# A norm summed in four column groups and spread by DMAs, and a silu gate, in a 16-stage network on one core

## The chip, the core and the metric

The kernel runs on one core of a Trainium2 chip. The metric is the device time of one execution in microseconds. The kernel before takes 4268.84 us, the median of three runs (4268.18 to 4270.52).

## The reference, cut to what matters

The reference sends an activation `x` of 16 sequences x 256 positions x 128 features, in fp32, through 16 residual stages: `x = x + stage(layernorm(x))`. The stages are, in order: a linear attention, a local layer, performer, the local layer again, linear, mixture of experts, decay, mixture of experts, causal linear, mix, window, mix, rope, adapters, ssm, adapters. Two of them matter here.

The local stage runs twice in the network, and each run has two layers:

```python
for layer in range(2):
    q, k, v = split(shift_token(x) @ wqkv)
    x = x + local_attention(rotary(l2norm(q)), rotary(l2norm(k)), v) @ wo   # windows of 64, the one before seen too
    h = shift_token(x)
    h = (h - h.mean(-1)) / sqrt(h.var(-1) + 1e-05) * lg + lb
    a, g = split(h @ w1 + b1)
    x = x + (a * gelu(g)) @ w2 + b2
```

The window stage is an attention with a sink (one more logit for each head in the softmax), and eight dense experts:

```python
h = h + attention(rmsnorm(h) * attn_norm_scale, sinks)
x = rmsnorm(h) * moe_norm_scale
gate = clip(gate_up[..., :INTER], NEG, 7.0);  up = clip(gate_up[..., INTER:], -7.0, 7.0)
out = sum over experts e of score[e] * ((up + 1) * gate * sigmoid(1.702 * gate)) @ down[e]
```

Every norm needs, for each position, a sum of squares over the 128 features.

## The kernel before, in words

Activations lie transposed in SBUF: the 128 features on the partitions and the 4096 positions along the free axis, in eight chunks of 512 (`NCH` is 8, `CH` is 512). Residual `x`, and the work arrays `ha` and `hb`, stay in SBUF for the whole program. All matmuls are fp32; the profile shows each of them as two passes, so it counts two matmuls for one call.

**A norm** has three steps, which the stages place where they like. `centre_step` (L1759) multiplies a chunk by the matrix `cent` and so subtracts the mean; the squares go to tile `nsq`, by GpSimd or by ScalarE. `spread_step` (L1774) multiplies `nsq` by the matrix `mean`, all of whose elements are 1/128. That sums over the partitions and at the same time leaves the sum on all 128 partitions. ScalarE then takes Ln and Exp(-0.5 x) of the whole 128x512 tile; the result is `nrs`, the factor 1/sqrt(variance + eps), on all partitions. With `twice` it makes two factors from one sum. The third step is a product on VectorE. `norm_x_step` (L1811) and `norm_of_half` (L3572) wrap these steps.

**The local layer** (`local_layer`, L3354) first calls `fill_rooms`, then `local_attend` and `local_ffn`. `local_attend` works through 32 half-sequence units, `m`; its order on each engine is the one written out in the loop at L3549 (`manual_schedule` keeps the emission order of every engine). One turn of `m` is called a slot here. `chunk_steps(m)` puts the norm steps in: for chunk c, `norm_of_half` does centre, spread, scale and bias in slots 4c+6 to 4c+9, for c below 7. In the first of two layers `norm_x_step` runs in slots 4c-9 to 4c-7, and only for chunks 5 to 7: the stage before has done the first five (`lead`, L1836). PSUM is shared as three banks `w`, four `s` and one `o`. `local_ffn` does the norm of chunk 7 in its turns 0 to 3 and then leads the next stage's norm.

**The rooms.** Both mixture-of-experts stages sort tokens into DRAM. `fill_rooms` (L2114) fills this memory once: 66 DMAs of up to 520 KB each and one of 64 KB, all issued by SP at the start of the first local layer.

**The window stage** (`window_attention`, L3163) has 128 units, n; the loop at L3327 starts at n = -14 with nothing but the norm of chunk 0. `before(c, i)` norms chunk c ahead of its projections, in slots 16c-14, 16c-12 and 16c-10, with two factors; `after(c, i)` norms the result for the experts, in slots 16c+24, +26 and +28. `prepare(0, 0)`, the first projections, comes at n = -8. Then `window_moe` (L2547) runs 64 units, eight experts for each of eight chunks: `wide` makes gate and up, `gate` multiplies them and the share `rb`, which ScalarE has copied from PSUM in `shares`, and `narrow` multiplies by `down`.

Weight loads for the next stage are issued by SP (`ahead`, L618) at the start of each stage and wait until the stage before is done with their buffer.

Of the kernel before, what the change touches and what calls it, by code (L numbers as in the profile page):

```python
# [1649 lines left out]
class Fast(Net):  # L1650
# [120 lines left out]
            self.gt(sq, dst, dst, ALU.mult)  # L1771
        return sq

    def spread_step(self, pool, sq, bank, eps="eps5", twice=False):  # L1774


        pv = self.bank(bank)
        self.mm(pv, self.k["mean"], sq)
        out = []
        for n in range(2 if twice else 1):  # L1780
            rs = pool.tile([P, CH], F32, tag=f"nrs{n}", name="nrs", bufs=2)
            if n:
                self.act(rs, pv, AF.Ln, scale=1.0 + 1e-5, bias=self.k["eps10"])
            else:
                self.act(rs, pv, AF.Ln, bias=self.k[eps])
            out.append(rs)
        for rs in out:
            self.act(rs, rs, AF.Exp, scale=-0.5)
        return out if twice else out[0]

    def norm_steps(self, pool, src, dst, bank, g=None, b=None, eps="eps5", copy=None, square=False):


        held = {}

        def centre():
            held[0] = self.centre_step(pool, src, dst, bank, copy, square)

        def spread():
            held[1] = self.spread_step(pool, held[0], bank, eps)  # L1800

        def scale():
            if g is None:
                self.tt(dst, dst, held[1], ALU.mult)
            else:
                self.stt(dst, dst, g, held[1], ALU.mult, ALU.mult)
                self.ts(dst, dst, b, ALU.add)

        return [centre, spread, scale]

    def norm_x_step(self, pool, c, i, bank="ps", copy=None):  # L1811

        if c in self.led:
            return
        if i == 0:
            s = self.chunk(c)
            self.norms[c] = self.norm_steps(pool, self.x[:, s], self.ha[:, s], bank, copy=copy)
        self.norms[c][i]()

    def slots(self, n, *steps, last=(), every=1):  # L1820
# [280 lines left out]
    def rooms(self, st):  # L2101


        nc = self.nc
        self.rows, self.many, self.filled = [], 0, False
        dram = st.enter_context(self.tc.tile_pool(name="dram", bufs=1, space=bass.MemoryType.DRAM))
        turns = sum(n == "moe_f" for n in self.loads)
        total = 8 * NT + WIDE
        for n in range(turns):
            self.rows.append(dram.tile([total, ROW], F32, tag=f"rows{n}", name="rows"))  # L2110
        if turns:
            self.back = dram.tile([2 * NT, C], F32, tag="back", name="back")

    def fill_rooms(self, st):  # L2114

        nc = self.nc
        if self.filled or not self.rows:
            return
        self.filled = True
        k = 8  # L2120
        t = self.stage(st, "fill", 1).tile([P, k, ROW], F32, tag="t", name="t")
        nc.gpsimd.memset(t, 0.0)
        nc.gpsimd.memset(t[:, :, C : C + 1].bitcast(I32), NOBODY)
        for rows in self.rows:
            n = rows.shape[0]
            for at in range(0, n, P * k):
                m = min(P * k, n - at) // P
                nc.sync.dma_start(rows[at : at + P * m].rearrange("(p a) d -> p a d", p=P), t[:, :m])
        nc.sync.dma_start(self.back[:P], t[:, 0, :C])

    def swiglu_moe(self, w):
        s = self.sending or self.send()
# [414 lines left out]
    def window_moe(self, w, h, n1):  # L2547

        x, nc = self.x, self.nc
        with ExitStack() as st:  # L2550
            p = self.stage(st, "e2", 1)
            compare, choose, turn = self.route_steps(st, w["gate"], 4, 0.25, w["gate_b"], "r")

            ub = p.tile([P, 16], F32, tag="ub", name="ub")
            self.ts(ub, w["gub"], 1.0, ALU.add)
            rts, rbs, gs, us, pos = {}, {}, {}, {}, {}

            def compared(c):
                self.logs(False)
                compare(c, n1)  # L2560

            def turned(c):
                rts[c] = turn(c)

            def shares(i):
                c, half = divmod(i, 2)
                rb = p.tile([P, 4, CH], F32, tag="rb", name="rb", bufs=2)
                for r, pb in enumerate(self.four(rts[c], self.k["sel4" + "ab"[half]], "r")):
                    self.act(rb[:, r], pb, AF.Copy)
                rbs[i] = rb  # L2570

            def wide(i):
                c, e = divmod(i, 8)
                s = self.chunk(c)
                pg, pu = self.bank(), self.bank()
                self.mm(pg, w["gu"][:, e * 256 : e * 256 + P], n1[:, s])
                self.mm(pu, w["gu"][:, e * 256 + P : e * 256 + 256], n1[:, s])
                g = p.tile([P, CH], F32, tag="g", name="g", bufs=4)
                u = p.tile([P, CH], F32, tag="u", name="u", bufs=6)
                sg = p.tile([P, CH], F32, tag="sg", name="sg", bufs=3)  # L2580
                self.ts(g, pg, w["gub"][:, 2 * e : 2 * e + 1], ALU.add, 7.0, ALU.min)
                self.act(sg, g, AF.Sigmoid, scale=1.702)
                self.ts(u, pu, ub[:, 2 * e + 1 : 2 * e + 2], ALU.add, 8.0, ALU.min)

                self.gt(g, g, sg, ALU.mult)
                gs[i], us[i] = g, u

            def gate(i):
                c, e = divmod(i, 8)
                self.stt(us[i], us[i], -6.0, gs.pop(i), ALU.max, ALU.mult)  # L2590
                self.gt(us[i], us[i], rbs[i // 4][:, e % 4], ALU.mult)

            def narrow(i):
                c, e = divmod(i, 8)
# [568 lines left out]
    def window_attention(self, w, h, n1, ns2):  # L3163
# [3 lines left out]
        with ExitStack() as st:  # L3167
# [134 lines left out]
            def before(c, i):  # L3302
# [2 lines left out]
                if i == 0:  # L3305
                    held["sq"] = self.centre_step(p1, self.x[:, s], h[:, s], "s", square=True)
                elif i == 1:
                    held["rs"] = self.spread_step(p1, held["sq"], "s", twice=True)
                else:
                    r1, r2 = held["rs"]  # L3310
                    self.stt(n1[:, s], h[:, s], w["ns1"], r2, ALU.mult, ALU.mult)
                    self.tt(h[:, s], h[:, s], r1, ALU.mult)

            def after(c, i):
# [3 lines left out]
                    held["sq"] = p1.tile([P, CH], F32, tag="nsq", name="nsq", bufs=2)  # L3318
                    self.act(held["sq"], h[:, s], AF.Square)
                elif i == 1:  # L3320
                    held["rs"] = self.spread_step(p1, held["sq"], "s")
                else:
                    self.stt(n1[:, s], h[:, s], ns2, held["rs"], ALU.mult, ALU.mult)

            with self.share(s=4, o=4), self.tc.manual_schedule():
                self.logs()
                for n in range(-14, len(units) + 16):  # L3327
                    if 0 <= n < len(units):
                        score(n)
                        later(n + 1, masked, n)  # L3330
# [10 lines left out]
                    i, rest = divmod(n - 14, 8)  # L3341
                    if rest == 0 and 0 <= i < 2 * NCH:
                        out(i)
                    c, u = divmod(n + 14, 16)
                    if u in (0, 2, 4) and c < NCH:
                        before(c, u // 2)
                    c, u = divmod(n - 24, 16)
                    if u in (0, 2, 4) and 0 <= c < NCH:
                        after(c, u // 2)

    def local_begin(self):
        pass
# [8 lines left out]
    def local_attend(self, w, z, hs, last):  # L3361
# [6 lines left out]
        with ExitStack() as st:  # L3368
# [158 lines left out]
            def chunk_steps(m):  # L3527
# [5 lines left out]
                if not last:  # L3533
                    for i in range(3):
                        if (c := due(i - 9)) is not None:
                            self.norm_x_step(p, c, i, "w")
                for slot in (-6, 5):
                    if (c := due(slot)) is not None:
                        self.shift(hs[:, self.chunk(c)], z[:, self.chunk(c)])
# [7 lines left out]
            with self.share(w=3, s=4, o=1), self.tc.manual_schedule():  # L3547
                self.logs()
                for m in range(-9, NTILE + 6):  # L3549
# [18 lines left out]
                    chunk_steps(m)  # L3568
                    if within(m + 5, NTILE):
                        project(m + 5)  # L3570

    def norm_of_half(self, pool, bank, w, s):  # L3572

# [3 lines left out]
            held[0] = self.centre_step(pool, s, s, bank)  # L3577

        def spread():
            held[1] = self.spread_step(pool, held[0], bank)  # L3580

        return [
            centre, spread, lambda: self.stt(s, s, w["lg"], held[1], ALU.mult, ALU.mult),
# [46 lines left out]
class Sending:  # L3630
# [3 lines left out]
    def __init__(self, net, rows):  # L3634
        self.net, self.rows, self.begun = net, rows, False
        self.stack = ExitStack()
        net.fill_rooms(self.stack)
        self.one = net.stage(self.stack, "g1", 1)
        self.p = net.stage(self.stack, "g2", 2)
        self.places = {-1: net.k["seg"]}  # L3640
# [208 lines left out]
```

## Time and profile before

| What | Value |
|---|---|
| Median of three runs | 4268.84 us |
| Profiled execution: its time / its span | 4291.23 us / 4289.4 us |
| Busy share of the span: PE, DVE, ACT, POOL | 91%, 61%, 54%, 45% |
| Mean granted TensorE clock | 0.949 |
| Local stage, its two runs, about | 115 to 840 us and 1130 to 1850 us of the span |
| Window attention, about | 2931 to 3407 us |
| Window experts, about | 3407 to 3654 us |

PE is TensorE's matmuls, PEld its weight loads, DVE VectorE, ACT ScalarE, POOL GpSimd and SP the engine that only issues DMAs. A row of the timeline gives start, duration, engine, line, operation, the tile written and the tiles read, the shape, a count when equal instructions are merged, and in brackets how long the engine was idle before it and what ended that. A matmul's shown duration includes the pipeline behind it, so the start of the next one says more than its end. A line such as L504 is a helper that many places call; the tile names say which place it is.

### The profile page before, as it was taken

How to read it: one execution, taken by the hardware profiler on the slowest of the kernel's cores; microseconds unless marked ns; L12 is line 12 of the kernel's file. 1: busy time of each engine (PE TensorE's matmuls, PEld its weight loads, DVE VectorE, ACT ScalarE, POOL GpSimd, SP SyncE). 2: the span in 40 equal slices, each digit the busy share in tenths (PEclk: the TensorE clock that was granted, in tenths of full speed). 3: DMA queues.
4: the chain of work that ended last, by engine and by line, in shares of the span. 5: the costliest groups of instructions: out<-in, count | busy, mean ns of one | idle time of the engine just before them, and what ended most of it. 6: DMA issues, size and time to landing. Idle time of an engine off the chain costs nothing. (4 is left out here: it accounts for less than half of the span.)

```text
span 4289.4 us, 73913 instructions
## 1 busy us (share of the span) xinstructions
PE 3886.8 (91%) x28998; PEld 2214.8 (52%) x28998; DVE 2597.7 (61%) x4503; ACT 2325.8 (54%) x4741; POOL 1949.6 (45%) x1696
## 2 busy tenths in 40 slices
PE   7999999998899999984989979888999999899978
PEld 3555466465465456553965549643444343455333
DVE  4775576374577377464336633555777698386474
ACT  6665466554766466552446634444555544674432
POOL 4664365232565166315433434454555498411251
PEclk8999999988999999997999979999999999999989
DMA  1800000000000000002930039100000000000000
GB/s 60 340 1 1 11 1 2 19 1 1 20 1 2 3 1 2 1 3 96 324 112 12 17 128 319 63 19 16 1 1 1 3 1 1 15 2 18 6 0 21
DMA packets 78404, 176.43 MB, mean 41 GB/s; under 512 B 12606, under 2 KB 39108, under 8 KB 77920
## 3 DMA queue, kind: packets, MB, share of 16 engines
q1 hardware_dynamic: 65568, 148.40, 10.0%
q0 software_dynamic: 9120, 18.51, 1.2%
q8 instruction: 231, 3.78, 0.4%
q10 hardware_dynamic: 3360, 4.72, 0.3%
q14 instruction: 125, 1.02, 0.1%
HBM read 118.28 MB, written 54.20 MB: 40 GB/s over the span
## 5 line engine op out<-in xcount | busy, mean ns | idle before, releaser
L528 ACT ACTIVATE pt<-ps 128x512 f32<-128x512 f32 x640 | 339.7, 600 | 325.1 <-PE ps L504 323.7
L504 PE MATMUL ps<-hb,w 128*128 128x512 f32 (+1 forms) x960 | 466.3, 619 | 8.8 <-issue 3.3
L504 PE MATMUL ps<-w,hb 128*128 128x512 f32 (+2 forms) x896 | 406.7, 575 | 25.4 <-DVE t L531 19.5
L534 POOL TENSOR_TENSOR t<-t,t 128x512 f32<-128x512 f32 x256 | 319.3, 1269 | 161.5 <-DVE t L531 101.5
L531 DVE TENSOR_TENSOR t<-ps,tab 128x512 f32<-128x512 f32 x512 | 317.6, 681 | 85.3 <-ACT sq L528 81.8
L534 POOL TENSOR_TENSOR t<-t,ss 128x1024 f32<-128x1024 f32 x128 | 243.5, 1903 | 218.7 <-ACT ss L528 217.5
L504 PEld LDWEIGHTS ps<-hb,w 128*128 128x128 f32 (+1 forms) x960 | 179.6, 192 | 270.5 <-issue 223.6
L528 ACT ACTIVATE qkt<-ps 128x512 f32<-128x512 f32 x256 | 140.5, 595 | 309.9 <-PE ps L508 309.3
L531 DVE TENSOR_TENSOR u<-u,ps 128x384 f32<-128x384 f32 (+1 forms) x206 | 121.8, 595 | 282.9 <-PE ps L504 122.4
L531 DVE TENSOR_TENSOR ot<-ps,rd 128x512 f32<-128x512 f32 (+2 forms) x224 | 143.3, 640 | 231.8 <-ACT rd L528 231.8
L534 POOL TENSOR_TENSOR nsq<-ha 128x512 f32<-128x512 f32 x112 | 123.1, 1099 | 322.0 <-ACT ha L528 305.0
L504 PEld LDWEIGHTS ps<-w,hb 128*128 128x128 f32 x896 | 156.8, 194 | 185.1 <-issue 115.4
L534 POOL TENSOR_TENSOR both<-pt 128x1024 f32<-128x1024 f32 x64 | 151.2, 2362 | 199.9 <-DVE pt L531 164.3
L504 PE MATMUL ps<-nsq,ct 128*128 128x512 f32 x368 | 203.6, 636 | 32.5 <-POOL nsq L534 27.6
L504 PE MATMUL ps<-ot,w 128*128 128x512 f32 x448 | 214.4, 613 | 17.3 <-DVE ot L531 9.2
L504 PE MATMUL ps<-u,w 128*128 128x512 f32 (+1 forms) x448 | 218.4, 611 | 8.4 <-POOL u L534 8.4
L2199 POOL DMA_INDIRECT back<-y,x x142 | 138.9, 978 | 185.5 <-ACT y L528 84.2
L504 PE MATMUL ps<-xt,w 128*128 128x128 f32 x1704 | 219.9, 279 | 1.7 <-ACT xt L528 1.5
L528 ACT ACTIVATE u<-ps,w 128x512 f32<-128x512 f32 x160 | 107.7, 685 | 183.1 <-PE ps L504 180.5
L504 PEld LDWEIGHTS ps<-xt,w 128*128 128x128 f32 x1704 | 203.7, 193 | 3.0 <-ACT xt L528 2.6
L3746 POOL DMA_INDIRECT rows<-out,idx x128 | 126.2, 986 | 170.2 <-ACT out L528 121.1
L528 ACT ACTIVATE nrs<-ps,ct 128x512 f32<-128x512 f32 x208 | 139.6, 683 | 103.2 <-PE ps L504 93.8
(363 smaller groups left out, 9095.3 us busy)
## 6 DMA issues: line engine op xcount, KB each, us to landing
w<-in_moe_x SPq DMA_DIRECT2D x142, 533.0 KB
rows<-t SPq DMA_DIRECT2D x64, 520.0 KB
x<-rows SPq DMA_DIRECT2D x142, 65.0 KB
w<-in_local_f SPq DMA_DIRECT2D x8, 659.5 KB
y<-back ACTq DMA_DIRECT2D x16, 256.0 KB
y<-back SPq DMA_DIRECT2D x16, 256.0 KB
w<-in_local_f SPq DMA_DIRECT2D x4, 658.5 KB
back<-y,x POOLq DMA_INDIRECT x142
```

Source lines behind the costliest of these rows:

```text
L504: self.nc.tensor.matmul(out, lhsT, rhs, start=start, stop=stop)
L528: self.nc.scalar.activation(out, in_, func, **kw)
L531: self.nc.vector.tensor_tensor(out, a, b, op)
L534: self.nc.gpsimd.tensor_tensor(out, a, b, op)
L2199: nc.gpsimd.indirect_dma_start(views[i], bass.IndirectOffsetOnAxis(ap=x[:, C : C + 1].bitcast(I32), axis=0), y, None, bounds_check=2 * NT ...
L3746: nc.gpsimd.indirect_dma_start(views[(c * 2 + k) * 4 + t], bass.IndirectOffsetOnAxis(ap=idx[:, k, t : t + 1], axis=0), out[:, k, t], None,)
```

## The change

Three things are changed.

First, `compact_spread`: the sum of squares is made by four matmuls with 32 columns of `mean`, each in its own column group of the array and each over a quarter of the chunk (128 positions). The quarter r lands on partitions 32r to 32r+31. ScalarE then takes Ln and Exp of 128x128 (of 128x128 twice and of 128x256 once with `twice`), into tile `nrow`. Four DMAs for each factor, issued by SP, read one row each, of partition 32r, and write it to all 128 partitions of `nrs`. It is used in the local layers (`norm_x_step` there, and `norm_of_half`) and in `before` and `after` of the window stage. The window's slots move: `before` in slots 16c-16, -14 and -10, `after` in 16c+24, +26 and +30, and the loop starts at n = -16.

Second, the DMAs that fill the rooms are put in a list, and SP issues two of them at the end of each slot of `local_attend`, in the first local layer.

Third, in the experts the gate is made by one Silu activation in place, silu(1.702 g) = 1.702 g sigmoid(1.702 g); the product on GpSimd and tile `sg` go away, and the factor 1/1.702 goes into the copy of `rb`.

```diff
+    def compact_spread(self, pool, sq, bank, eps, twice):
+        nc = self.nc
+        pv = self.bank(bank)
+        for r in range(4):
+            nc.tensor.matmul(
+                pv[32 * r : 32 * r + 32, :P], self.k["mean"][:, :32], sq[:, r * P : r * P + P],
+                start=True, stop=True, skip_group_check=True,
+            )
+        many = 2 if twice else 1
+        rows = pool.tile([P, many, P], F32, tag="nrow", name="nrow", bufs=2)
+        self.act(rows[:, 0], pv[:, :P], AF.Ln, bias=self.k[eps])
+        if twice:
+            self.act(rows[:, 1], pv[:, :P], AF.Ln, scale=1.0 + 1e-5, bias=self.k["eps10"])
+        flat = rows.rearrange("p n t -> p (n t)")
+        self.act(flat, flat, AF.Exp, scale=-0.5)
+        out = []
+        for n in range(many):
+            rs = pool.tile([P, CH], F32, tag=f"nrs{n}", name="nrs", bufs=2)
+            for r in range(4):
+                nc.sync.dma_start(rs[:, r * P : r * P + P], rows[32 * r : 32 * r + 1, n][:, None].broadcast_to([1, P, P]))
+            out.append(rs)
+        return out if twice else out[0]
...
-                nc.sync.dma_start(rows[at : at + P * m].rearrange("(p a) d -> p a d", p=P), t[:, :m])
-        nc.sync.dma_start(self.back[:P], t[:, 0, :C])
+                self.fills.append((rows[at : at + P * m].rearrange("(p a) d -> p a d", p=P), t[:, :m]))
+        self.fills.append((self.back[:P], t[:, 0, :C]))
+
+    def fill_some(self, n):
+        for out, t in self.fills[:n]:
+            self.nc.sync.dma_start(out, t)
+        del self.fills[:n]
...
-                    self.act(rb[:, r], pb, AF.Copy)
+                    self.act(rb[:, r], pb, AF.Copy, scale=1.0 / 1.702)
...
-                sg = p.tile([P, CH], F32, tag="sg", name="sg", bufs=3)
                 self.ts(g, pg, w["gub"][:, 2 * e : 2 * e + 1], ALU.add, 7.0, ALU.min)
-                self.act(sg, g, AF.Sigmoid, scale=1.702)
+                self.act(g, g, AF.Silu, scale=1.702)
                 self.ts(u, pu, ub[:, 2 * e + 1 : 2 * e + 2], ALU.add, 8.0, ALU.min)
-
-                self.gt(g, g, sg, ALU.mult)
...
-                for n in range(-14, len(units) + 16):
+                for n in range(-16, len(units) + 16):
...
-                    c, u = divmod(n + 14, 16)
-                    if u in (0, 2, 4) and c < NCH:
-                        before(c, u // 2)
+                    c, u = divmod(n + 16, 16)
+                    if u in (0, 2, 6) and c < NCH:
+                        before(c, (u + 1) // 3)
                     c, u = divmod(n - 24, 16)
-                    if u in (0, 2, 4) and 0 <= c < NCH:
-                        after(c, u // 2)
+                    if u in (0, 2, 6) and 0 <= c < NCH:
+                        after(c, (u + 1) // 3)
...
                     if within(m + 5, NTILE):
                         project(m + 5)
+                    self.fill_some(2)
+                self.fill_some(len(self.fills))
```

The calls of `spread_step` in `norm_x_step` of the local layer, in `norm_of_half`, and in the window's `before` and `after` get `compact=True`; all other norms stay as they were.

More of the change, by code (lines that the diff above doesn't have):

```diff
@@ L1772, in centre_step, with spread_step @@
         return sq
-    def spread_step(self, pool, sq, bank, eps="eps5", twice=False):
+    def spread_step(self, pool, sq, bank, eps="eps5", twice=False, compact=False):
+        if compact:
+            return self.compact_spread(pool, sq, bank, eps, twice)
         pv = self.bank(bank)
@@ L1789, in spread_step, with norm_steps @@
         return out if twice else out[0]
-    def norm_steps(self, pool, src, dst, bank, g=None, b=None, eps="eps5", copy=None, square=False):
+    def compact_spread(self, pool, sq, bank, eps, twice):
[20 more added lines that the diff above has]
+        return out if twice else out[0]
+    def norm_steps(self, pool, src, dst, bank, g=None, b=None, eps="eps5", copy=None, square=False, compact=False):
         held = {}
@@ L1799, in spread @@
         def spread():
-            held[1] = self.spread_step(pool, held[0], bank, eps)
+            held[1] = self.spread_step(pool, held[0], bank, eps, compact=compact)
         def scale():
@@ L1809, in norm_steps, with norm_x_step @@
         return [centre, spread, scale]
-    def norm_x_step(self, pool, c, i, bank="ps", copy=None):
+    def norm_x_step(self, pool, c, i, bank="ps", copy=None, compact=False):
         if c in self.led:
@@ L1816, in norm_x_step @@
             s = self.chunk(c)
-            self.norms[c] = self.norm_steps(pool, self.x[:, s], self.ha[:, s], bank, copy=copy)
+            self.norms[c] = self.norm_steps(pool, self.x[:, s], self.ha[:, s], bank, copy=copy, compact=compact)
         self.norms[c][i]()
@@ L2104, in rooms @@
         nc = self.nc
-        self.rows, self.many, self.filled = [], 0, False
+        self.rows, self.many, self.filled, self.fills = [], 0, False, []
         dram = st.enter_context(self.tc.tile_pool(name="dram", bufs=1, space=bass.MemoryType.DRAM))
@@ L2119, in fill_rooms @@
         self.filled = True
+        self.fills = []
         k = 8
@@ L3307, in before @@
                 elif i == 1:
-                    held["rs"] = self.spread_step(p1, held["sq"], "s", twice=True)
+                    held["rs"] = self.spread_step(p1, held["sq"], "s", twice=True, compact=True)
                 else:
@@ L3320, in after @@
                 elif i == 1:
-                    held["rs"] = self.spread_step(p1, held["sq"], "s")
+                    held["rs"] = self.spread_step(p1, held["sq"], "s", compact=True)
                 else:
@@ L3535, in chunk_steps @@
                         if (c := due(i - 9)) is not None:
-                            self.norm_x_step(p, c, i, "w")
+                            self.norm_x_step(p, c, i, "w", compact=True)
                 for slot in (-6, 5):
@@ L3579, in spread @@
         def spread():
-            held[1] = self.spread_step(pool, held[0], bank)
+            held[1] = self.spread_step(pool, held[0], bank, compact=True)
         return [
@@ L3637, in __init__ @@
         net.fill_rooms(self.stack)
+        net.fill_some(len(net.fills))
         self.one = net.stage(self.stack, "g1", 1)
```

## The prediction

> **What bounds the kernel now.** I read the page first, then busy time by stage, then the timeline of one slot in each stage that the change touches. Busy time by stage (start:end, length, then busy us and count of PE, PEld, DVE, ACT, POOL, the granted clock, DMA):
>
> ```profile
> 520.00:745.00 225.00, 221.38 (x2279) 139.96 (x2276) 163.99 (x248) 147.74 (x397) 137.30 (x121) 1.00 0.01 2
> 2957.00:3400.00 443.00, 441.94 (x3438) 181.08 (x3436) 351.57 (x552) 231.30 (x508) 244.99 (x141) 1.00 0.00 1
> 3420.00:3643.00 223.00, 215.91 (x617) 91.75 (x615) 202.05 (x279) 109.35 (x174) 200.40 (x150) 0.97 0.00 1
> 3643.00:3654.00 11.00, 4.76 (x8) 1.87 (x8) 3.73 (x4) 1.74 (x2) 8.74 (x10) 0.69 0.00 0
> ```
>
> Local attention (first row) and window attention (second) are TensorE's: 98% and nearly 100%. In the experts (third) PE, DVE and POOL are all at 90% or more; in their tail (fourth) POOL alone works.
>
> One local slot, from the timeline (start, duration):
>
> ```profile
> 599.73 1.02 PE L504 MATMUL ps<-nsq,ct 128*128 128x512 f32 x2
> 600.59 1.88 PE L504 MATMUL ps<-w,hb 128*128 128x512 f32 x4
> 602.57 0.67 ACT L528 ACTIVATE nrs<-ps,ct 128x512 f32<-128x512 f32 x1
> 603.27 0.63 ACT L528 ACTIVATE nrs<-nrs 128x512 f32<-128x512 f32 x1
> 604.27 0.40 PE L3490 MATMUL ps<-pu,v 128*32 128x128 f32 x8
> 604.49 0.51 PE L3490 MATMUL ps<-pt,v 128*32 128x192 f32 x8
> 605.61 0.40 PE L3490 MATMUL ps<-pu,ct 128*32 128x128 f32 x8
> 605.95 1.09 PE L508 MATMUL ps<-ct,t 128*128 128x128 f32 x8
> 611.14 2.30 DVE L543 SCALAR_TENSOR_TENSOR hb<-hb,w,nrs 128x512 f32<-128x512 f32 x1
> ```
>
> The first row is the sum to be replaced: 600.59 - 599.73 = 0.86 us of PE. Rows 5 to 8 are the form that replaces it, eight matmuls (four column groups, two passes) of 128 columns: 0.22 us to the next of their kind, 0.34 to one over the whole array. The factor is ready at 603.90 and used at 611.14: 7.2 us of cover.
>
> Where there is less: the end of a local layer, the start of window attention, and the nearest DMA in size (64 KB from DRAM, issue to use).
>
> ```profile
> 766.74 0.63 ACT L528 ACTIVATE nrs<-nrs 128x512 f32<-128x512 f32 x1
> 769.98 0.74 DVE L543 SCALAR_TENSOR_TENSOR hb<-hb,w,nrs 128x512 f32<-128x512 f32 x1
> 772.14 0.69 DVE L531 TENSOR_TENSOR ha<-ha,ps 128x512 f32<-128x512 f32 x1 [1.42 <-PE ps L504]
> 772.88 5.42 PE L504 MATMUL ps<-hb,w 128*128 128x512 f32 x12 [0.78 <-DVE ha L531]
> ...
> 2936.28 1.15 ACT L528 ACTIVATE nrs<-nrs 128x512 f32<-128x512 f32 x2
> 2937.54 0.75 DVE L543 SCALAR_TENSOR_TENSOR hb<-ha,w,nrs 128x512 f32<-128x512 f32 x1 [4.93 <-ACT nrs L528]
> ...
> 2020.17 0.01 SPq L2165 DMA_DIRECT2D x<-rows  x1
> 2021.41 0.45 PE L508 MATMUL ps<-ct,x 128*128 128x128 f32 x1 [25.16 <-DMA x<-rows]
> ```
>
> [...] eight matmuls take the time of two, and leaving the mode costs 0.12 us. [...] The trace of before has no DMA that reads one partition. [...] the product `u<-u,g` takes 0.68 us at least, 1.17 in the median and 1.74 at most.
>
> **The change part by part.**
>
> *Sums.* 54 spreads change: 28 of `norm_of_half` in attention (seven chunks, four layers), 4 in the FFNs, 6 of `norm_x_step`, 16 in the window. Each gives back 0.86 us of PE and takes 0.22, plus 0.12 to leave the mode and about 0.07 to enter it: saved 0.45. Bounds 0.36 and 0.64 (no or double mode cost). 54 x 0.45 = 24 us; 19 to 35.
>
> *ScalarE.* 0.67 + 0.63 us become about 0.3 + 0.3 (a 128x128 `pu` takes 0.22 to 0.28). ACT isn't the bound, but in the six `norm_x` slots PE waits up to 0.73 us for `ha`, which stands behind this work: -2 us.
>
> *DMAs.* Everything hangs on L, the time from the end of Exp to the landing of the last of four DMAs. Issue is 0.33 us each on SP. Fixed cost: 2020.17 to 2021.41 is 1.24 us, of which about 0.2 is transfer. [...] L = 6.0[...] L = 10.8. [...] (512 B packets take about 0.03 us, eight for each engine and DMA): L = 3. With `twice` there are eight DMAs, and the first product wants the second factor: 10.8, 20.4 and 4.3. I take 6.0 and 10.8[...].
>
> *Where L is covered.* Local slots: 7.2 us, plus 0.7 by which Exp ends earlier, plus 1.5 that the product now loses[...] (2.30 instead of 0.74): 9.4. FFN turn: 7.5. Window slots: two slots are 6.0 us (3106.2 to 3112.2), with two more of 3.4 and the shorter ACT about 13. All hold at 6.0 and 10.8; without this cover VectorE would stall, and with it the projections' products behind, which free PE's `w` banks.
>
> *Where it isn't.* (a) Layer end: VectorE's order has the product ahead of the last `ha<-ha,ps`, and PE's first FFN matmul waits for that. With Exp ending at about 766.4, landing at 772.4, then 0.74 + 0.69, PE starts at about 773.9 instead of 772.9: +1 us in each of four layers, +4. (b) Window start: nothing else runs. Exp ends about 2935.7; plus 10.8 is 2946.5 against 2937.5: +9. The load of 1.6 MB ahead of it on SP's queue (issued 2931.9) is through by then. (c) Window end: the product for chunk 7 goes from 3409.9 to about 3414.4; it stands among the router's short VectorE operations, and PE waits for these until 3414.2. Between 0 and +4.5: +2.5.
>
> *Slots of the window.* Two more empty slots at the start add nothing but (b). Each SP issue ahead of others costs SP 1.3 us a spread; SP has nothing else due there.
>
> *Fills.* Before, they run from 117 to 206 us and local slots beside them take the same 7.19 us as in layer two, so the stream is hidden and stays so. SP's first spread comes at m = 7; the 32 fills ahead of it need 32 x 1.32 us (64 took 84.7), done by about 163 us, and slot 7 is near 200. Later two fills (2.6 us) lie between spreads at least 7 us apart: 0. If they delayed a landing, it would be by 2.6 us, inside the cover.
>
> *Silu.* 64 products of 1.26 us or more leave POOL; ACT's count, and its table loads, stay. The loop takes 28.1 us a chunk. PE's own work in it, counted at 0.43 us a pass, is 25.2 (26.9 with the lead's norm), so at most 5 x 1.2 + 3 x 2.9 = 15 us can go, and VectorE (17.4 us of long operations, 6 of router and sums, and what is still lost to GpSimd) stands close behind at some 25.7. I take half, 7.5. Tail: POOL's last products end about 4.5 us earlier: -4.5. Together -12, bounds -4 and -20.
>
> Sum: -24 - 2 + 4 + 9 + 2.5 - 12 = -22.5 us. The profiled execution took 4291.23 us (span 4289.4), 0.5% above the median; -22.5 x 0.995 is still -22.4, so **4246 us**.
>
> **The rivals.**
>
> *Fast landing* ([...]L = 3 and 4.3). For it: DRAM loads of this size land in 1.24 us. Against: their source isn't one partition. Then (a) is 0, (b) +2.4, (c) +1: -24 - 2 + 3.4 - 12 = -34.6, **4234 us**.
>
> *Slow landing* (the slower side). [...] At L = 10.8 and 20.4: layer ends 4 x 5.8 = 23; local slots 30 x 1.4 x 0.9 = 38; FFN turns 7; window start 18.5; window loop, 7 chunks x 7.4 us late x 0.7 = 36; end 4. 127 - 38 = +89, 4357 us. At L = 9.4 (18 with eight): 18 + 16 + 23 + 4 - 38 = +23, **4292 us**. It decides at L = 8 (14.8 with eight): 12 + 13 + 9 + 3.5 balances the 38 saved. [...]
>
> *Thin gain*: VectorE takes POOL's place in the experts (it is at 202 of 223 us), and mode changes cost double. -19 - 4 + 15.5 = -8, **4261 us**. The change would do what it says and be worth little.
>
> **How the numbers follow.** Chances: main 0.42, fast landing 0.24, thin gain 0.10, slow landing 0.24. What a measurement here can tell from no change is about 0.2%, 8.5 us. Main and fast are faster: 0.66; thin is the same: 0.10; slow: 0.24. The main case's own range is 4236 to 4260 (its terms' bounds). The range reaches below the fast case to 4226, with the upper bound of the sums, and above into the slow one to 4310, which leaves out its worst part, about 0.1, and as much or less below.
>
> **What would show it.** L itself: the wait of SP's four issues on ACT and the landing of `nrs`. VectorE's product should show no new wait for a DMA in local slots (right), or one of over a microsecond (slow). Local slots with a spread shorten by 0.45 us. Between mix and window PE should be idle 9 us longer. In the experts `u<-u,g` should come down towards 0.7 to 0.9 us and POOL to about half; a chunk should take about 27.1 us. The forecast is wrong if landings take over 8 us, or if eight column matmuls take as long as two over the whole array.

## The result and the profile after

The changed kernel takes 4290.31 us (median of seven runs, 4284.19 to 4302.84); the kernel before takes 4270.52 us in seven runs (4268.18 to 4277.04). The ratio is 1.0045, with a 95% interval of 1.0033 to 1.0058: the change makes the kernel slower by some 20 us. The forecast was 4246 us, faster.

Busy time by stage of the changed kernel, for stretches that hold the same work as the first three rows shown of before (the columns are the same: start and end, length, busy us and count of PE, PEld, DVE, ACT, POOL, granted clock, DMA share, GB/s):

```profile
520.00:745.00 225.00, 217.64 (x2262) 136.69 (x2262) 157.00 (x249) 144.85 (x397) 137.44 (x123) 1.00 0.12 7
2974.00:3417.00 443.00, 439.78 (x3496) 180.76 (x3498) 350.00 (x551) 219.60 (x500) 243.25 (x139) 0.99 0.23 14
3437.00:3643.00 206.00, 205.70 (x614) 90.55 (x613) 163.18 (x280) 112.16 (x176) 104.97 (x88) 0.99 0.00 1
```

The first two stages are still TensorE's. The third has changed: the same work fits in 206 us in place of 223, POOL falls from 200 us to 105, and VectorE from 202 to 163.

One local slot, from the timeline of the changed kernel:

```profile
603.05 0.42 PE L1798 MATMUL ps<-nsq,ct 128*32 128x128 f32 x8
603.40 1.98 PE L504 MATMUL ps<-w,hb 128*128 128x512 f32 x4
...
605.80 0.35 ACT L528 ACTIVATE nrow<-ps,ct 128x128 f32<-128x128 f32 x1
606.18 0.31 ACT L528 ACTIVATE nrow<-nrow 128x128 f32<-128x128 f32 x1
606.52 3.84 SPq L1813 DMA_DIRECT2D nrs<-nrow  x4
...
616.53 0.75 DVE L543 SCALAR_TENSOR_TENSOR hb<-hb,w,nrs 128x512 f32<-128x512 f32 x1 [2.71 <-DMA nrs<-nrow]
...
620.52 0.67 DVE L531 TENSOR_TENSOR ha<-ha,ps 128x512 f32<-128x512 f32 x1
```

The sum now takes 603.40 - 603.05 = 0.35 us of TensorE in place of 0.86, as it should. But the factor, which left ScalarE at 606.49, is used at 616.53, and VectorE stood idle for 2.71 us until the DMA brought it. L, counted to the start of the product, is 10.0 us; the forecast's main case had 6.0. The wait delays `ha<-ha,ps`, and PE waits for that: over the whole kernel PE waits for `ha` 48.1 us in 27 waits, where it waited 14.8 us in 12. Of the 48.1 us, 23.2 are four waits at the layer ends and 11.1 are 14 waits of 0.7 to 0.9 us in the slots, of which the kernel before has none.

The layer's end, and the window's start, in the same view:

```profile
770.62 0.31 ACT L528 ACTIVATE nrow<-nrow 128x128 f32<-128x128 f32 x1
770.95 3.92 SPq L1813 DMA_DIRECT2D nrs<-nrow  x4
...
781.06 0.75 DVE L543 SCALAR_TENSOR_TENSOR hb<-hb,w,nrs 128x512 f32<-128x512 f32 x1 [6.49 <-DMA nrs<-nrow]
782.46 8.18 PE L504 MATMUL ps<-hb,w 128*128 128x512 f32 x12 [5.86 <-DVE ha L531]
...
2936.89 0.42 ACT L528 ACTIVATE nrow<-nrow 128x256 f32<-128x256 f32 x1
2937.33 10.44 SPq L1813 DMA_DIRECT2D nrs<-nrow  x8
2953.96 0.75 DVE L543 SCALAR_TENSOR_TENSOR hb<-ha,w,nrs 128x512 f32<-128x512 f32 x1 [19.59 <-DMA nrs<-nrow]
```

At the layer's end L is 781.06 - 770.93 = 10.1 us, and PE's idle time ahead of the FFN's first matmul grows from 0.78 to 5.86 us. One more thing is seen there: the twelve passes that follow take 8.18 us, and before they took 5.42. The clock that was granted to TensorE was half of the full one there, as the view by stretches shows (the third figure from the end):

```profile
782.50:787.50 5.00, 5.00 (x6) 2.14 (x7) 0.75 (x1) 2.04 (x3) 1.28 (x3) 0.50 0.00 0
```

At the window's start, with eight DMAs, L is 2953.96 - 2937.31 = 16.7 us; what it costs there is in the table below.

VectorE's product in the experts, in the changed kernel (count, duration in ns: least, median, most):

```profile
L543 DVE SCALAR_TENSOR_TENSOR u<-u,g x64: 677/681/1298, 3443.9 to 3645.6; 128x512 f32<-128x512 f32 x64
```

It takes 0.68 us in the median, where it took 1.17 (678/1168/1742 for the same 64 products of before). Of those of before, the ten with no work of GpSimd beside them took 0.68 to 0.69 us, and the other 54 between 0.68 and 1.74, 1.27 in the median.

The trace of before was of an execution some 20 us above its median, and so the two traces have nearly the same span. A second trace of the kernel before (4270.5 us, told of below) serves for the comparison by stage. This table gives the length of each stage, taken between the starts of the same VectorE instructions in each trace; the kernels in it are those of the experiments.

| us | Local run 1 | Local run 2 | Window's start | Window, rest | Experts |
|---|---|---|---|---|---|
| before, second trace | 718.8 | 707.8 | 15.5 | 464.7 | 247.0 |
| changed | 734.0 | 719.7 | 31.3 | 467.2 | 227.7 |
| Silu alone | 715.9 | 706.1 | 16.8 | 464.9 | 228.6 |
| plain sums where nothing covers L | 716.1 | 701.7 | 15.5 | 470.9 | 228.1 |
| other order of DMAs | 723.1 | 706.3 | 27.1 | 465.2 | 227.8 |
| rows 36 apart | 717.7 | 703.3 | 24.4 | 463.1 | 227.7 |
| 32 rows a DMA | 709.6 | 698.0 | 20.3 | 463.5 | 227.9 |
| 32 rows, window's chunk 0 plain | 712.6 | 698.0 | 15.5 | 464.2 | 228.4 |
| 32 rows, window plain | 709.3 | 698.2 | 15.5 | 464.2 | 228.7 |

Changed against before: +15.2, +11.9, +15.8, +2.5 and -19.3, together +26 us, where the spans of the two traces differ by 18 and the medians by 20. The other 8 us lie in stages that the change doesn't touch. Executions differ by such amounts: the first local run moves by 3 us between two traces of one kernel (712.6 and, in a repeat, 709.6), and the stretch between the two local runs, which no edit touches, takes 278 to 293 us in these traces.

### The profile page after: what moved, and what is told of

The parts are those of the page before. It is cut to its first block, busy times and chain, and to the rows that moved or that the text cites. A ratio compares the mean times of both kernels' runs of the same rounds, so it can differ in the third digit from the quotient of the medians.

```text
span 4288.5 us, 75028 instructions
## 1 busy us (share of the span) xinstructions
PE 3841.4 (90%) x29322; PEld 2195.0 (51%) x29322; DVE 2524.1 (59%) x4503; ACT 2291.8 (53%) x4733; POOL 1851.7 (43%) x1632
## 3 DMA queue, kind: packets, MB, share of 16 engines
q14 instruction: 129, 1.06, 0.1%
## 5 line engine op out<-in xcount | busy, mean ns | idle before, releaser
L504 PE MATMUL ps<-hb,w 128*128 128x512 f32 (+1 forms) x960 | 469.6, 623 | 44.7 <-DVE ha L531 23.2
L504 PE MATMUL ps<-ha,w 128*128 128x512 f32 x320 | 174.6, 667 | 14.8 <-ACT f L528 10.2
L531 DVE TENSOR_TENSOR pt<-ps,w 128x384 f32<-128x384 f32 (+1 forms) x320 | 170.5, 573 | 17.7 <-PE ps L504 11.8
```

The costliest lines, as they stand in the source:

```text
L504: self.nc.tensor.matmul(out, lhsT, rhs, start=start, stop=stop)
L531: self.nc.vector.tensor_tensor(out, a, b, op)
```

## The experiments

The author's theory after the traces: the four DMAs take 10 us because each reads a single partition, one DMA after another, and the cost sits where no other work covers 10 us. The rival: the cost is in the slots, in SP's stream or in the number of packets, and the silu gain is smaller than it looks.

**Silu alone.** The kernel before, with the third part of the change only:

```diff
-                    self.act(rb[:, r], pb, AF.Copy)
+                    self.act(rb[:, r], pb, AF.Copy, scale=1.0 / 1.702)
...
-                sg = p.tile([P, CH], F32, tag="sg", name="sg", bufs=3)
...
-                self.act(sg, g, AF.Sigmoid, scale=1.702)
+                self.act(g, g, AF.Silu, scale=1.702)
...
-                self.gt(g, g, sg, ALU.mult)
```

> The kernel before, with nothing changed but the experts' gate (one Silu in place, the product on GpSimd gone, 1/1.702 in the copy of the share). Theory A (read from the two traces: between 3420 and 3654 us of the span the lag of the changed kernel behind the one before falls from 18 us to -1.6 us): the experts give 20 us, and the kernel takes about 4250 us; a chunk of eight experts takes about 26 us in place of 28.1. Rival B (the prediction's number): 12 us, about 4258 us; part of the 20 us would then be some other effect, such as work that waited behind the late window.

Measured: 4253.76 us (4252.21 to 4257.12), ratio 0.9954, interval 0.9941 to 0.9968. That is 19.5 us below its runs of before: theory A. The experts take 228.6 us in place of 247.0. It follows that the rest of the change, the compact sums and the spread-out fills, costs about 40 us.

**Four DMAs that read 32 partitions each.** All 32 rows of a column group hold the same sums, so a DMA can read them all, four times each:

```diff
-                nc.sync.dma_start(rs[:, r * P : r * P + P], rows[32 * r : 32 * r + 1, n][:, None].broadcast_to([1, P, P]))
+                nc.sync.dma_start(rs[:, r * P : r * P + P], rows[32 * r : 32 * r + 32, n][:, None].broadcast_to([32, 4, P]))
```

> The changed kernel, but each of the four DMAs of a factor reads 32 partitions (32r to 32r+31, which all hold the same sums) four times each, in place of one partition 128 times. Same number of DMAs, of packets and of bytes. Theory A[...] L (end of Exp to the landing of the last of four) falls from 10.0 us to about 4 us, which is issue and fixed cost; layer ends lose nothing, the window's start loses about 6 us in place of 16, and the local slots keep the 0.9 us of each spread: about 4230 us. Rival B (the four DMAs are held by their packets, by their writes or by SP's issue): L stays near 10 us and the time near 4290 us.

Measured: 4237.62 us (4233.61 to 4239.69), ratio 0.9914, interval 0.9900 to 0.9927. This one line turns a loss of 20 us into a gain of 36 against its own runs of before. L is 4.2 us with four DMAs. With eight it is 6.8 us, as the window's start shows:

```profile
2897.44 0.42 ACT L528 ACTIVATE nrow<-nrow 128x256 f32<-128x256 f32 x1
2897.88 5.11 SPq L1813 DMA_DIRECT2D nrs<-nrow  x8
2904.67 0.75 DVE L543 SCALAR_TENSOR_TENSOR hb<-ha,w,nrs 128x512 f32<-128x512 f32 x1 [9.74 <-DMA nrs<-nrow]
```

What was moved is the same, 64 KB in 128 rows of 512 B; what changed is how many partitions it is read from. GB/s in 40 slices of 16 us (one spread of the changed kernel, from 604 us) and of 12 us (one of this kernel, from 755 us), from the view of the DMAs:

```profile
GB/s 0 0 0 0 0 41 0 0 0 29 26 31 26 26 31 24 27 31 23 32 106 37 24 31 22 28 22 30 24 65 3 0 0 0 0 20 0 0 0 0
```

```profile
GB/s 0 0 0 0 27 0 0 9 149 62 121 97 96 123 68 149 2 0 0 0 0 0 0 0 0 0 0 0 0 0 0 0 0 0 0 0 0 0 0 0
```

The changed kernel moves 22 to 32 GB/s for most of 8.4 us, this one 62 to 149 GB/s in the eight slices (2.4 us) that carry nearly all. A rival that lays L to the number of packets or to the writes is out, since these are the same in both kernels (576 packets and 0.26 MB in each of these views). What differs is how long a packet takes: the packets fill 31.5% of the 16 engines' time in the first view and 9.2% in the second, 0.14 us and 0.03 us each.

**Four rows that lie 36 apart.**

```diff
-                nc.sync.dma_start(rs[:, r * P : r * P + P], rows[32 * r : 32 * r + 1, n][:, None].broadcast_to([1, P, P]))
+                nc.sync.dma_start(rs[:, r * P : r * P + P], rows[36 * r : 36 * r + 1, n][:, None].broadcast_to([1, P, P]))
```

> The changed kernel, but the four DMAs read partitions 0, 36, 72 and 108 in place of 0, 32, 64 and 96[...]. Theory A[...]: L stays at 9 to 10 us, 4283 to 4293 us. Rival B (all four DMAs' reads are open at once[...], as the prediction's main case had it): L falls to about 5 us, and the time to about 4235 us.

Measured: 4254.88 us (4253.81 to 4266.61), ratio 0.9962, interval 0.9949 to 0.9976; L is 6.9 us (10.9 with eight). Neither theory: L lies between. The DMAs do overlap, but not all the time. The view of the DMAs over 12 us, from 761 us:

```profile
GB/s 0 0 0 0 27 0 0 29 29 27 26 27 27 58 156 99 73 97 58 48 29 27 26 24 14 0 0 0 0 0 0 0 0 0 0 0 0 0 0 0
```

For its first 1.8 us the transfer goes at 26 to 29 GB/s and for its last 1.5 us at 14 to 29, and between at 48 to 156, where DMAs overlap. That asks whether it is which rows are read or which DMAs stand next to each other.

**The same rows in another order.**

```diff
-            for r in range(4):
+            for r in (0, 2, 1, 3):
                 nc.sync.dma_start(rs[:, r * P : r * P + P], rows[32 * r : 32 * r + 1, n][:, None].broadcast_to([1, P, P]))
```

> The changed kernel with its own four rows, 0, 32, 64 and 96, but the DMAs issued in the order 0, 64, 32, 96[...]. Theory A[...]: L falls from 10.0 us to about 7 us[...], and the time to about 4256 us. Rival B[...] L about 10 us, 4290 us.

Measured: 4263.49 us (14 runs, 4249.49 to 4273.67), ratio 0.9970, interval 0.9961 to 0.9979. L is 7.5 us, and 12.3 with eight. Theory A in L: no row and no byte is different, only which DMA follows which. Over its 8.4 us the changed kernel, in the order 0, 32, 64, 96, goes above 37 GB/s only in the middle, where row 64 follows row 32 (the slice of 106), and in one slice at its end (65). This one has, in its view of the DMAs from 763 us, 68, 82, 79, 60, 53 and 50 GB/s in six slices of 0.3 us in a row, behind the first 1.8 us at 27 to 31, and 67 and 91 in two later ones. So the reads of rows 0 and 32 did not overlap, and those of 0 and 64 did. That two rows lie on two partitions is not enough, since 0 and 32 are two partitions as 0 and 64 are; what sets the pairs apart was not shown. The time is 7 us above what theory A gave, and spread over 24 us; the run after next bears on a part of that.

**Plain sums where nothing covers L.** In each local layer the sum for chunk 6, and in the window that for chunk 0, are made as before:

```diff
-                            steps[1] = self.norm_of_half(p, "w", w, hs[:, self.chunk(c)])
+                            steps[1] = self.norm_of_half(p, "w", w, hs[:, self.chunk(c)], compact=c < NCH - 2)
...
-                    held["rs"] = self.spread_step(p1, held["sq"], "s", twice=True, compact=True)
+                    held["rs"] = self.spread_step(p1, held["sq"], "s", twice=True, compact=c > 0)
```

> The changed kernel, but the sum for chunk 6 in each local layer (the one at the layer's end) and the one for chunk 0 of the window stage are made as in the kernel before, on all partitions by TensorE; 49 of 54 stay as changed. Theory A (the loss sits at the five places where nothing covers L): the four layer ends give back 4 x 7.2 us and the window's start 16 us, less 5 x 0.5 us of sums, 42 us in all: about 4248 us. Rival B (the loss is spread over the slots, by SP's stream or by late products): at most 10 us come back, 4280 us or more.

Measured: 4252.66 us (4249.55 to 4253.46), ratio 0.9948, interval 0.9934 to 0.9961. Theory A: five places of 54 hold 37.6 of the 40 us that the compact sums cost. But what is left then gains nothing against Silu alone (4253.76). By the table its local runs are 4 us shorter than with Silu alone, and the rest of its window is 6 us longer, and 3.7 us longer than the changed kernel's, which isn't explained.

**TensorE kept at work during the wait.** Behind the last output projection of each local layer:

```diff
+                busy = self.bank("w")
+                for _ in range(6):
+                    self.mm(busy, self.k["mean"], w["w1"][:, :CH])
```

These six matmuls are added work, whose result nobody reads.

> The changed kernel, with six more matmuls of 128x512 (12 passes, 5.2 us at full clock) at the end of each local layer, behind the last output projection; nobody reads their result. TensorE then works in the 6.4 us for which it waits for the last factor. Theory A (beyond the wait itself, TensorE's clock is at half for up to 6.8 us after it: the first six or seven passes of the FFN take 0.85 us in place of 0.43): the FFN starts when it did, but at full clock; 3 x 2.6 + 1.6 = about 9 us come back, 4281 us. Rival B (the slow passes have another cause, such as the weights' first use): 4290 us or a little more.

Measured: 4282.99 us (4270.56 to 4288.68), ratio 1.0024, interval 1.0013 to 1.0034, against 1.0045 (1.0033 to 1.0058): 7 to 9 us come back with more work done. PE alone, at the same layer end:

```profile
776.60 5.31 PE L504 MATMUL ps<-w,ct 128*128 128x512 f32 x12
782.57 5.42 PE L504 MATMUL ps<-hb,w 128*128 128x512 f32 x12 [0.66 <-DVE ha L531]
```

The FFN starts at 782.57, as in the changed kernel (782.46), but takes 5.42 us in place of 8.18. So the wait of 5.9 us costs 2.8 us more than its length. The added matmuls read the FFN's first weights, so this run alone doesn't rule out rival B; the granted clock does, with 1.00 here from 782.6 to 787.6 us and 0.50 in the changed kernel.

In the trace of the changed kernel the granted clock is 1 or 0.5 throughout, in stretches of 3.41 us and multiples of it (all but the last of 110). Counted in windows of 3.41 us over that whole trace, it fell to half after all 41 windows at full clock in which PE was busy for less than 45% of the time, 28 of them at less than 37%; after 8 of the 37 with 45 to 60%; and after 6 of the 1053 with more. The first trace of the kernel before has 37 of 37, 9 of 32 and 11 of 1056. So it also matters where a wait lies in the windows. With 5.8 us of idle PE (the changed kernel) the clock is at half behind all four layer ends. With 3.1 to 3.3 us (other order) it is so behind two, behind one in part, and not behind one. With 2.5 to 2.7 us (rows 36 apart) it is so behind one of four. Two of the other order:

```profile
773.19 8.25 PE L504 MATMUL ps<-hb,w 128*128 128x512 f32 x12 [3.26 <-DVE ha L531]
```

```profile
1439.51 5.42 PE L504 MATMUL ps<-hb,w 128*128 128x512 f32 x12 [3.12 <-DVE ha L531]
```

This can be only a part of the 24 us over which that kernel's runs are spread. The traced execution is the slowest of the 14 and loses 7.4 us so at its layer ends (2.9, 2.8 and 1.7), so without any such loss it would still take 4266 us, where the fastest takes 4249. The mean granted clock is 0.954 in the three fastest runs and 0.945 and 0.948 in the two slowest; where else it falls in them is not known, as only one was traced.

**The fills first.** All DMAs of the rooms at the start of the first local layer, as before:

```diff
         self.fills.append((self.back[:P], t[:, 0, :C]))
+        self.fill_some(len(self.fills))
```

> The changed kernel with all 67 DMAs of the rooms issued at once at the start of the first local layer, as in the kernel before. Theory A (SP has time for two fills a slot): no difference, 4288 to 4293 us. Rival B (the fills, spread over the first layer, stand between the four DMAs of a factor and lengthen L there): the first layer's slots with the output projection are 0.7 us longer than the other layers', seven times, so 4 to 6 us come back: 4285 us.

Measured: 4294.72 us (4277.34 to 4305.40), ratio 1.0054, interval 1.0042 to 1.0067. No gain: theory A. In its trace the slots of the first layer, from 115 to 385 us, stay within 0.8 us of the changed kernel's. The traced execution, the fastest of the six, has its first local run 7 us shorter all the same, all of it between 385 and 440 us. In this kernel eight of the twelve FFN passes at the end of the first layer come ahead of the wait for `ha`, which is 2.61 us there in place of 5.77, and the clock doesn't fall behind it. So the edit did move something else, at one layer end, and the median shows no gain from it.

**32 rows, and the window's chunk 0 plain.** The edit of the 32 rows shown above, and in `before`:

```diff
-                    held["rs"] = self.spread_step(p1, held["sq"], "s", twice=True, compact=True)
+                    held["rs"] = self.spread_step(p1, held["sq"], "s", twice=True, compact=c > 0)
```

> The changed kernel with DMAs that read 32 partitions, as the run before it of that kind (4237.6 us), and in the window stage the sum for chunk 0 made as in the kernel before. Theory A: with eight DMAs L was still 7.1 us there, and between the traces of the kernel with Silu alone and of that run the window's start loses 3.5 us; they come back, 4234 us. Rival B: the loss at the start is made up later in the window anyway; no change, 4237 us.

Measured: 4233.69 us (4227.97 to 4243.13), ratio 0.9908, interval 0.9895 to 0.9921. The window's start is 15.5 us again in place of 20.3 (L with eight DMAs was 6.8 us by the lines above, not 7.1). Against 0.9914 for 32 rows alone the times don't tell the two apart; the stage does.

**32 rows, and the whole window plain.** The edit of the 32 rows, and in `before` and `after`:

```diff
-                    held["rs"] = self.spread_step(p1, held["sq"], "s", twice=True, compact=True)
+                    held["rs"] = self.spread_step(p1, held["sq"], "s", twice=True)
...
-                    held["rs"] = self.spread_step(p1, held["sq"], "s", compact=True)
+                    held["rs"] = self.spread_step(p1, held["sq"], "s")
```

> The changed kernel with DMAs that read 32 partitions, and in the window stage all 16 sums made as in the kernel before (the slots stay as changed). Against the run with only chunk 0 made so (4233.7 us), 15 column-group sums of the window are taken back. Theory A (in the trace each of them takes 0.50 us less of TensorE, but the packed score matmuls that follow take 0.41 us more, so they are worth 0.1 us each): 4235 us, no difference that shows. Rival B (the prediction's price, 0.45 us each): 15 x 0.45 = 7 us, 4240.5 us.

Measured: 4241.96 us (4237.03 to 4244.10), ratio 0.9929, interval 0.9916 to 0.9943: by the time, rival B. The two traces say otherwise: the rest of the window takes 464.2 us in both. The two kernels had run on different chips, so both ran again, side by side on one.

> The same kernel as the one with DMAs that read 32 partitions and only chunk 0 of the window summed as before, now on the same chip and in the same rounds as the next one. Theory A (a window sum by column groups is worth 0.1 us: in the two traces the window takes the same time to 0.3 us): within 3 us of the next one. Rival B (it is worth 0.45 us or more, as the 8 us between the two medians, taken on different chips, would say): 7 us or more below it.

> The same kernel as the one with DMAs that read 32 partitions and all 16 sums of the window as before. Theory A: within 3 us of the one above, both at 4233 to 4241 us. Rival B: 7 us or more above it.

Measured: 4232.33 us (4231.15 to 4237.14), ratio 0.9909, interval 0.9894 to 0.9924, with chunk 0 plain; 4236.35 us (4230.84 to 4242.03), ratio 0.9925, interval 0.9912 to 0.9939, with the whole window plain. They differ by 4 us, between the two theories, and the intervals overlap. In the second pair of traces the rest of the window is 464.2 and 464.4 us. So fifteen sums are worth nothing in the window itself. In both pairs the kernel with the plain window is about 2 us longer after the experts, in stages that no edit touches; so is the kernel with the other order, whose window sums are compact. Why is not known, and what makes the medians differ stays open. The timeline of PE shows where the sums' gain goes; first the plain window, then the compact one:

```profile
3097.67 1.02 PE L504 MATMUL ps<-nsq,ct 128*128 128x512 f32 x2
3098.62 1.13 PE L504 MATMUL ps<-q,k 64*128 64x512 f32 x4
3099.68 1.70 PE L3290 MATMUL ps<-pt,v 128*32 128x256 f32 x25
```

```profile
3091.74 0.61 PE L3290 MATMUL ps<-both,ct 128*32 128x256 f32 x8
3092.29 1.13 PE L504 MATMUL ps<-q,k 64*128 64x512 f32 x4
3093.35 1.98 PE L504 MATMUL ps<-hb,w 128*128 128x512 f32 x4
...
3095.26 0.42 PE L1798 MATMUL ps<-nsq,ct 128*32 128x128 f32 x8
3095.62 1.54 PE L504 MATMUL ps<-q,k 64*128 64x512 f32 x4
3097.09 1.72 PE L3290 MATMUL ps<-pt,v 128*32 128x256 f32 x28
...
3123.11 0.29 PEld L504 LDWEIGHTS ps<-q,k 64*128 64x128 f32 x2 [0.26 <-ACT nrow L528]
```

The sum takes 0.36 us in place of 0.95, and the score matmuls after it (`ps<-q,k`) take 1.47 in place of 1.06. The account that was expected, that such matmuls lose time behind a group of column tiles, is not borne out: in the first rows of the compact window the scores follow column tiles too (`both,ct`) and take 1.06 us, as all 58 such groups of this trace do. What holds the scores behind a sum is a wait. In 14 places scores follow a compact sum. In six of them the second score matmul is released by VectorE's `q` (3095.92 in the place shown; in the plain window the same release comes 0.2 us before the scores begin), and the scores take 1.47 us. In six it is released by ScalarE's first Ln of the sum (the last row), and they take 1.61 (the other two take 1.50 and 1.87). So of the 0.59 us that TensorE saves, 0.41 or 0.55 goes into waiting for the other two engines.

**The kernel before, once more**, with no edit.

> The kernel before once more, for a second trace of it. The trace shown first is of an execution of 4291 us, 20 us above its median, and its stages between 1930 and 2500 us take 20 us longer than the same stages in the changed kernel, which doesn't touch them. Theory A: that is that one execution; the second trace spans about 4270 us and has these stages as the changed kernel has them. Rival B: the changed kernel makes them faster; the second trace is as the first there.

Measured: 4272.27 us, span 4270.5. The stages between 1930 and 2570 us are 23 us shorter than in the first trace, and as in the changed kernel: theory A.

## Why the prediction was wrong

The step that failed is the transfer. The forecast took L = 6.0, with two DMAs at work at once all the time; that was the author's estimate, as was the 10.8 of the slow landing, and no trace of before showed either. L is 10.0 us, and 16.7 with eight: the reads of rows 0 and 32, the first two in the queue, did not overlap, nor those of 64 and 96 (22 to 32 GB/s). Several DMAs can overlap (rows 36 apart: slices of 73 to 156 GB/s); but here that was so only for some neighbours in the queue. The forecast named the slower side as the slow landing, which decides at L = 8. The order of the four DMAs stood in the diff; which neighbours would overlap was shown only by the experiments.

That the slow landing's 4292 us (for L = 9.4) lies next to the measured 4290 is luck. At the measured L of 10.0 and 16.7 the same prices give 20 + 16 + 15 + 18 + 4 - 38 = +35 us, some 4304. At a smaller L they did better. With L = 4.2 and 6.8 (32 rows) they give about -32 us, and the kernel is 36 us below its runs of before. With 6.9 and 10.9 (rows 36 apart) they give about -19, and it is 18 below. With 7.5 and 12.3 (other order) they give about -15, and it is 12 below. So the places where L is uncovered were right, while some terms were off against each other. By the steps:

- *Sums, -24.* Half right. TensorE's own time falls as priced. In the middle of a local layer a chunk of four slots, with one sum, takes 33.76 us with 32 rows and 34.34 before: 0.58 for the sum, ScalarE's share included. Over the local runs 38 sums give 14.4 us against Silu alone (715.9 - 709.6 and 706.1 - 698.0), 0.38 each, with the 3 us by which executions differ. In the window 16 sums give nothing, where 7 us were counted: the price of leaving the mode, 0.12 us, wasn't the fault, but the forecast took all that TensorE saves as won, and there it waits for VectorE and ScalarE instead.
- *Layer ends, +4.* Measured about 30: at the one shown PE's wait is 5.1 us longer and the passes after it take 2.8 us more; so at three of them, and at the first 5.1 and 1.6 us (7.01 us for the twelve passes). By the forecast's own formula L = 10.0 gives 20. The other 10 are the clock, which it didn't count.
- *Local slots, 0.* The local runs take 46 us more than with 32 rows; less 30 at the layer ends, some 16 are in the slots, 11 of them PE's 14 waits for `ha`. The cover was 8.8 us, not 9.4: with 32 rows VectorE comes to the product 7.24 us after Exp without waiting, and takes 2.30 for it, where behind a wait it takes 0.75. L = 10.0 is 1.2 us beyond that, and 0.7 to 0.9 of it reach PE.
- *Window's start, +9.* Measured 15.8; the step was right, with L for eight DMAs 5.9 us too short.
- *Window's loop.* VectorE waits for the factor seven times, 20.3 us in all, as the cover of 13 us said it would at this L; PE loses 2.5 us, where slow landing counted 0.7 of each wait.
- *Window's end, +2.5.* VectorE waits 5.8 us for the last factor, but nothing is lost: the experts take 227.7 us, and 227.9 with 32 rows.
- *Fills, 0.* Right, as far as the runs can tell.
- *Silu, -12.* Measured -19.5, near the bound of -20. The mechanism was right: POOL at 105 us, `u<-u,g` at 0.68. VectorE did not stand close behind: its busy time fell by 39 us, most of it in this product (64 x 0.49 us by the medians), and PE is now busy for 205.7 of 206 us.
- *SP's issue, 0.33 us each.* It is 0.6 us in the median and up to 3.4 (1.7 with 32 rows): the four issues of a spread end 3.9 us after Exp, and with 32 rows 2.5. It is a part of L that the forecast took for small, and 2.5 of the 4.2 us that stay pass before the last issue is done.

The measured terms, 30 + 16 + 16 + 2.5 - 14 - 19, give +31; the stages of the traces give +26 and the medians +20. Of the 5 us between the first two, nearly all come from the reference: the 14 are counted against Silu alone, whose local runs, which its edit doesn't touch, were 4.6 us shorter in its trace than those of before. The rest lies in the stages that weren't changed, as said under the table.

## What to carry to other kernels

Here DMAs that each spread one partition's row to all others moved 22 to 32 GB/s where they did not overlap, and neighbours in the queue overlapped only for some pairs of rows (0 and 64, but not 0 and 32); DMAs that read 32 partitions each brought L from 10.0 us to 4.2. Where many partitions hold the same values, read from all of them. Before work is moved from TensorE to DMAs, list the places where nothing covers the landing: here 5 of 54 held nearly the whole loss. A wait of TensorE can cost more than its length, since the clock may be down when it goes on: here it was at 0.50 behind all four layer-end waits of 5.8 us of the changed kernel, where the one shown cost 2.8 us more than its length, and at half behind some of 2.5 to 3.3 us in two other kernels. And time that TensorE saves is won only where no other engine stands close behind: the window's sums gave nothing.

## What was not expected of the hardware

- Four DMAs of 64 KB, each from one partition, take 8.4 us from the first packet to the last in the order of rows 0, 32, 64, 96; the same four in the order 0, 64, 32, 96 land 2.6 us earlier (L 7.5 for 10.1 at the layer's end).
- The eight issues of one spread take SP 10.4 us with one row a DMA and 5.1 with 32, and a single one took up to 3.4 us (1.7 with 32 rows). So the issue seems to be held up when the DMAs ahead are slow.
- TensorE's clock fell to half without a whole idle window: in the trace of the changed kernel after all 41 windows of 3.41 us at full clock with PE busy for less than 45%, and after 14 of the 1090 with 45% or more.
